# The rounded high parts of q and k made by ScalarE instead of VectorE

## The chip, the cores and the metric

The kernel runs on one core of a Trainium2 chip. The core has five engines with a queue each: TensorE (PE: matrix products, with weight loads shown apart as PEld), VectorE (DVE), ScalarE (ACT), GpSimd (POOL) and SyncE (SP), which here issues the DMA transfers. Each engine takes its instructions in the order in which they are written; between engines they wait for each other by semaphores. The metric is the device time of one execution in microseconds, as the median of several runs. One further execution was recorded by the hardware profiler; its rows carry the reasoning.

## The reference

The input x is 8 sequences of 1024 tokens with 512 features, float32. Out of one layer norm two branches are fed, and both are added to x:

```python
xn = _layernorm(x, axis=-1)
x = x + _L0_attn_ref(xn, W_attn, b_attn, W_proj, b_proj) + _L0_ffn_ref(xn, w_gate, w_up, w_down)
```

The attention has 16 heads of 32 features and is causal:

```python
qkv = x @ W_attn + b_attn
q, k, v = jnp.split(qkv, 3, axis=-1)
att = jnp.einsum('bhqd,bhkd->bhqk', q, k) * HD ** (-0.5)
att = jnp.where(causal[None, None], att, -jnp.inf)
att = jax.nn.softmax(att, axis=-1)
y = jnp.einsum('bhqk,bhkd->bhqd', att, v)
return y @ W_proj + b_proj
```

The feed-forward branch (512 to 1408 to 512) first rounds both operands of each product to 4-bit floats in blocks of 16 with a scale each: `h = silu(fp4_linear(x, w_gate)) * fp4_linear(x, w_up)`, then `fp4_linear(h, w_down)`.

## The kernel before, in words

**Tiles.** Tokens are taken in 64 tiles of 128 (class Tile). Attention is done in 64 units (class Unit): two heads (HU) of one sequence, all 1024 queries. A bank is one of six accumulators of 128x512 in PSUM (class Banks); two further accumulators, y and acc, hold sums of the attention and of the feed-forward branch.

**Stages.** `prepare` takes two tiles at a time (QT = 2): it normalises them (`normed`, VectorE and GpSimd), turns them on TensorE (`transposed`, L351; ScalarE copies the result to xnT, L352) and calls `project`. `weights_quantised` rounds the three weight matrices of the feed-forward branch and turns them; the rounding itself (class `Quantised`, L320 to L344) is on VectorE. These run at the start: the preparation of the first 16 tiles (AHEAD) beside most of the weights. After that six streams are merged until the end: `weigh` (the attention itself), `maxima` (row maxima and sums of one unit ahead), the feed-forward `network`, `quantised` (its input tiles), the remaining preparations, and `finish` (output projection and sum).

**The projection of q and k.** For each pair of tiles `project` makes, for q and for k (s), two steps of two blocks of 128 features (f): 16 products on TensorE into one bank (L466), then two ScalarE operations of 128x256 that add the bias, scale q, and write the tile `full` in SBUF (L478). So there are 4 steps for a pair and 128 in all. Each step ends with a split: q and k are kept as two parts that add up, `high` (rounded to float32r, a float32 type of fewer mantissa bits that TensorE multiplies) and `low` (the remainder, also written as float32r, over `full`). Both parts go to DRAM (`store`, L497, on SyncE), and `load_half` loads them again as `qs` and `ks`, of which the products of `maxima` (L597) and `weigh` (L727) are made. The two steps for v in `project` write their copy into a tile that is also named `full` (L522). Both `full` and `high` have two buffers (pool p2), and a buffer can be written again when the store from it has landed.

**The split.** VectorE makes `high` by a copy with conversion (L491) and then `low = full - high` (L492). The split isn't written where the step is, but later: `stored.append(Later(end - clock[0] - 0.3, split))`, where `end` is the planned end of the second ScalarE operation; `settle(stored)` in the next step writes whatever is still outstanding before a new `full` is taken. The two stores follow the same way.

**What sets the order.** The program is written out at build time by a planner. It has a clock of its own, and for ScalarE, VectorE and GpSimd a time at which each will be free (`free`). `act(columns, after)` and `dve(us, after)` add an operation to these accounts: ScalarE is charged 0.17 us and 0.00083 us per column, VectorE the number of microseconds given; `after` is the time before which the operation can't start, to which HOP = 0.2 us is added. `Later` objects are due at a planned time and are written when the clock passes it. `merge` picks the stream whose next step can start soonest, by the planned time of its inputs and by `banks.when`, the planned time at which enough banks come free. `maxima` also waits for `free["dve"] - QUEUE` (L629). So a changed charge can change the order in which the program's instructions are written, on every engine.

**Releases.** A bank used by `maxima` is released by ScalarE's exponential with a sum (L568), one used by `weigh` by the exponential L735, one of the projection by L478 or L522.

Of the kernel before, what the change touches and what calls it, by code (L numbers as in the profile page):

```python
# [27 lines left out]
def kernel(  # L28
# [31 lines left out]
    nc = tc.nc  # L60
# [14 lines left out]
    W = QG * P  # L75
# [69 lines left out]
    def on(engine, us, after=0.0):  # L145

        free[engine] = max(free[engine], clock[0], after + HOP) + us
        return free[engine]

    def act(columns, after=0.0, function="other"):  # L150
        if function == "other":
            function = table[0]
        switch = TABLE if function != table[0] else 0.0
        table[0] = function
        return on("act", 0.17 + 0.00083 * columns + switch, after)

    def dve(us, after=0.0):
        return on("dve", us, after)
# [275 lines left out]
    def settle(entries):  # L434
        while entries:
            entries.pop(0).now()
# [16 lines left out]
    def project(batch, xnT, g, after, first):  # L453
        yield 0.0, after, 1
        for s in range(2):
            for f in range(0, NC, 2):
                if first:
                    halves = [w[:, :, :] for w in resident_a[s * NC + f : s * NC + f + 2]]
                else:
                    wa = ring_a.take()  # L460
                    halves = [wa[:, :, j * P : (j + 1) * P] for j in range(2)]
                k, bank = banks.take()
                pq = bank.rearrange("p (j t) -> p j t", j=2)
                for j in range(2):
                    for c in range(NC):
                        nc.tensor.matmul(  # L466
                            pq[:, j, :],
                            lhsT=halves[j][:, c, :],
                            rhs=xnT[:, c, :],
                            start=(c == 0),  # L470
                            stop=(c == NC - 1),
                        )
                if not first:
                    ring_a.load_in(3.44 + HOP)
                settle(stored)
                full = p2.tile([P, 2, QW], F32, name="full")
                for j in range(2):
                    nc.scalar.activation(  # L478
                        full[:, j, :],
                        pq[:, j, :],  # L480
                        AF.Identity,
                        bias=bqk[:, s, f + j : f + j + 1],
                        scale=SCALE if s == 0 else 1.0,
                    )
                    end = act(QW, clock[0] + 1.7 * (j + 1))
                banks.back(k, end)
                high = p2.tile([P, 2, QW], F32R, name="high")
                low = full.bitcast(F32R)

                def split(full=full, high=high, low=low):  # L490
                    nc.vector.tensor_copy(high, full)  # L491
                    nc.vector.tensor_tensor(low, full, high.bitcast(F32), ALU.subtract)  # L492
                    dve(1.15)

                def store(s=s, f=f, high=high, low=low):
                    for piece, part in ((0, high), (1, low)):
                        nc.sync.dma_start(  # L497
                            out=batch.qk[s, piece, f : f + 2, :, g * QW : (g + 1) * QW].rearrange("f p t -> p f t"),
                            in_=part.bitcast(F32),
                        )  # L500

                stored.append(Later(end - clock[0] - 0.3, split))
                stored.append(Later(end - clock[0] + 2.0, store))
                yield 3.44, 0.0, 1
        for f in range(0, NC, 2):
            wa = resident_a[2 * NC + f // 2] if first else ring_a.take()
            k, bank = banks.take()
            pv = bank.rearrange("p (i t) -> p i t", i=QT)
            for i in range(QT):
                for c in range(NC):  # L510
                    nc.tensor.matmul(  # L511
                        pv[:, i, :],
                        lhsT=xnT[:, c, i * P : (i + 1) * P],
                        rhs=wa[:, c, :],
                        start=(c == 0),
                        stop=(c == NC - 1),
                    )
            if not first:
                ring_a.load_in(3.44 + HOP)
            settle(stored)  # L520
            v_out = p2.tile([P, QT, 2 * P], F32, name="full")
            nc.scalar.copy(v_out, pv)  # L522
            end = act(W, clock[0] + 3.44)
            banks.back(k, end)

            def store(f=f, v_out=v_out):
                nc.sync.dma_start(
                    out=batch.v[g * QT : (g + 1) * QT, :, f * P : (f + 2) * P].rearrange("t p e -> p t e"), in_=v_out
                )

            stored.append(Later(end - clock[0] + 0.5, store))
            yield 3.44, 0.0, 1
# [650 lines left out]
```

## Time and profile before

| | |
|---|---|
| median of 3 runs | 4255.48 us (4254.81 to 4258.41) |
| the profiled execution's own time | 4251.42 us |
| its span, first to last instruction | 4249.7 us |
| granted TensorE clock, mean | 0.991 |
| the 128 casts L491 | 54.8 us busy, 428 ns each |
| the 128 subtractions L492 | 89.3 us busy, 697 ns each |
| the 256 operations L478 | 107.4 us busy, 470 ns each |

The profile names an operation by its line in the kernel, its engine, and what it writes and reads ("high<-full"). "bank L597 <- ACT bank L568: 16.2, 49, 1.6" in the list of waits says that operations of line 597 stood idle before they started, until line 568 on ScalarE was done: 16.2 us in total, 49 times, 1.6 us the longest. In the timeline a row gives the start, the length, the engine, the operation and, in brackets, the idle time of the engine before it and what ended it. In the table of stretches each engine has its busy time and the number of its instructions. Idle time of an engine that isn't the bound costs nothing, and the busy time of TensorE is not a measure of its peak.

### The profile page before, as it was taken

To read this page: it belongs to the slowest core of one execution; us is meant where nothing else is said; L and a number is where in the kernel's file an instruction comes from. 1 tells how busy PE (TensorE), PEld (TensorE's weight loads), DVE (VectorE), ACT (ScalarE), POOL (GpSimd) and SP (SyncE) were. 2 spreads that over 40 slices of the span, in tenths; PEclk is the share of its full clock that TensorE was granted. 3 is DMA by queue.
4 is the path that set the end of the run, shared out by engine and by line. 5 is a ranking of instruction groups with operands and counts; after the bars stand their busy time and mean duration, and the time that the engine had idled before them with its cause. 6 is when DMAs were issued, how large, how long until landed. Compare 5 with 4: busy or idle time off the path is not lost.

```text
span 4249.7 us, 58555 instructions
## 1 busy us (share of the span) xinstructions
PE 4131.2 (97%) x17684; PEld 2619.1 (62%) x17684; DVE 2763.2 (65%) x7323; ACT 2321.8 (55%) x5918; POOL 546.5 (13%) x1296
## 2 busy tenths in 40 slices
PE   7789999999999999999999999999999999999998
PEld 6666666666666666666666666666666555555555
DVE  6786765666575666575666575666565666667755
ACT  2246556565555565555565555565555666666640
POOL 0001111111111111111111111111111111111110
PEclk9889999999999999999999999999999999999999
DMA  5654434455455455455455455455454433333314
GB/s 183 177 173 129 124 103 120 118 157 157 132 155 150 140 164 153 132 156 151 140 160 155 134 154 149 141 162 153 138 149 131 117 92 94 95 92 93 93 56 126
DMA packets 564187, 573.84 MB, mean 135 GB/s; under 512 B 114976, under 2 KB 420128, under 8 KB 563872
## 3 DMA queue, kind: packets, MB, share of 16 engines
q1 hardware_dynamic: 563872, 570.10, 48.3%
q8 instruction: 142, 2.33, 0.2%
q14 instruction: 173, 1.42, 0.1%
HBM read 400.56 MB, written 169.35 MB: 134 GB/s over the span
## 4 chain that ended last, share of the span: by engine, by line
PE 82%; ACT 7%; DVE 4%; DMA 1%; issue 1%; SPq 0%; ACTq 0%; POOL 0%; DVEq 0%
PE bank L831 26%; PE acc L809 12%; PE bank L466 8%; PE y L706 7%; PE bank L724 6%; PE bank L727 6%; PE bank L597 5%; PE bank L936 5%; PE bank L511 4%; ACT bank L568 3%; PE bank L351 2%; ACT L568 1%; ACT L843 1%; ACT pr L735 1%; DMA ks<-y_kept 1%
## 5 line engine op out<-in xcount | busy, mean ns | idle before, releaser
L568 ACT ACTIVATE bank<-bank,neg 128x512 f32<-128x512 f32 (+3 forms) x1536 | 856.7, 559 | 163.7 <-DVE neg L610 119.8
L735 ACT ACTIVATE pr<-bank 128x512 f32<-128x512 f32 (+3 forms) x1536 | 662.7, 494 | 482.6 <-PE bank L727 478.2
L741 POOL TENSOR_SCALAR_AFFINE_SELECT pr<-pr 128x128 f32<-128x128 f32 x1024 | 393.2, 397 | 3238.3 <-ACT pr L735 3228.9
L610 DVE CUSTOM_DVE_ANT_0 bank<-bank,mask 128x128 f32<-128x128 f32 (+3 forms) x1024 | 501.2, 500 | 469.5 <-PE bank L597 455.7
L724 PE MATMUL bank<-shT,pick 128*128 128x512 f32 (+3 forms) x1536 | 683.8, 453 | 2.7 <-DVE hid L848 1.5
L831 PE MATMUL bank<-wuT,xqT 128*128 128x512 f32 (+1 forms) x1536 | 676.1, 565 | 3.9 <-ACT bank L568 1.0
L809 PE MATMUL acc<-wdT,hqT 128*128 128x512 f32 x1408 | 665.4, 596 | 1.3 <-ACT hqT L352 1.3
L831 PE MATMUL bank<-wgT,xqT 128*128 128x512 f32 (+1 forms) x1536 | 662.9, 561 | 0.0
L597 PE MATMUL bank<-ks,qs 128*128 128x512 f32 (+3 forms) x1536 | 636.2, 475 | 24.7 <-ACT bank L568 21.7
L727 PE MATMUL bank<-qs,ks 128*128 128x512 f32 (+3 forms) x1536 | 516.9, 346 | 0.0
L622 DVE TENSOR_REDUCE neg<-bank 128x1 f32<-128x512 f32 x512 | 345.7, 685 | 186.8 <-PE bank L597 185.6
L597 PEld LDWEIGHTS bank<-ks,qs 128*128 128x128 f32 x1536 | 277.5, 191 | 234.1 <-issue 111.3
L831 PEld LDWEIGHTS bank<-wuT,xqT 128*128 128x128 f32 x1536 | 277.0, 190 | 228.8 <-issue 158.9
L831 PEld LDWEIGHTS bank<-wgT,xqT 128*128 128x128 f32 x1536 | 280.0, 190 | 219.3 <-issue 151.9
L724 PEld LDWEIGHTS bank<-shT,pick 128*128 128x128 f32 x1536 | 290.4, 189 | 155.7 <-issue 78.9
L809 PEld LDWEIGHTS acc<-wdT,hqT 128*128 128x128 f32 x1408 | 255.3, 190 | 197.0 <-issue 183.6
L478 ACT ACTIVATE full<-bank,bqk 128x256 f32<-128x256 f32 x256 | 107.4, 470 | 491.1 <-PE bank L466 409.3
L727 PEld LDWEIGHTS bank<-qs,ks 128*128 128x128 f32 x1536 | 290.6, 189 | 110.6 <-issue 77.1
L466 PE MATMUL bank<-xnT,wa 128*128 128x256 f32 x1536 | 349.8, 381 | 0.9 <-ACT xnT L352 0.6
L466 PEld LDWEIGHTS bank<-xnT,wa 128*128 128x128 f32 x1536 | 288.4, 190 | 55.6 <-issue 18.9
L706 PE MATMUL y<-pr,vs 128*32 128x512 f32 (+3 forms) x3072 | 316.5, 501 | 0.8 <-POOL pr L741 0.8
L568 ACT ACTIVATION_READ_ACCUMULATOR bank<-bank,neg 128x1 f32 x1536 | 315.4, 205 | 0.0
(99 smaller groups left out, 4674.7 us busy)
## 6 DMA issues: line engine op xcount, KB each, us to landing
wa<-in_L_attn_W_attn_dram SPq DMA_DIRECT2D x146, 512.0 KB
qs<-qk_kept SPq DMA_DIRECT2D x512, 128.0 KB
ks<-qk_kept SPq DMA_DIRECT2D x512, 128.0 KB
wp<-in_L_attn_W_proj_dram SPq DMA_DIRECT2D x81, 512.0 KB
qk_kept<-high SPq DMA_DIRECT2D x128, 256.0 KB
qk_kept<-full SPq DMA_DIRECT2D x128, 256.0 KB
y_kept<-yu SPq DMA_DIRECT2D x256, 128.0 KB
yT<-y_kept SPq DMA_DIRECT2D x112, 256.0 KB
```

The source lines that it names most:

```text
L466: nc.tensor.matmul(pq[:, j, :], lhsT=halves[j][:, c, :], rhs=xnT[:, c, :], start=(c == 0), stop=(c == NC - 1),)
L568: nc.scalar.activation(part, part, AF.Exp, bias=neg[:, kind, k + j : k + j + 1], scale=1.0 if kind == 1 else -1.0, accum_out=sums[:, kind, ...
L597: nc.tensor.matmul(sc[:, j * n : (j + 1) * n], lhsT=un.qs[Q][:, r, i * P : (i + 1) * P], rhs=un.ks[h][:, r, :n], start=True, stop=True,)
L610: nc.vector.tensor_tensor_reduce(part, part, mask[:, W - n :], scale=-1.0, scalar=3e38, op0=ALU.add, op1=ALU.min, accum_out=neg[:, kind, k ...
L622: nc.vector.tensor_reduce(neg[:, kind, k : k + 1], sc[:, :n], AX.X, ALU.max, negate=True)
L706: nc.tensor.matmul(y[row : row + HD, q0:], lhsT=un.vs[h][:, jj, r * HD : (r + 1) * HD], rhs=pr[:, q0:], start=(j < 2), stop=(j >= last - 1 ...
L724: nc.tensor.matmul(w[:, q0:], lhsT=pick[:, Q * HU + r, :], rhs=un.shT[:, q0:], start=True, stop=False)
L727: nc.tensor.matmul(w[:, q0:], lhsT=un.ks[h][:, r, jj * P : (jj + 1) * P], rhs=un.qs[Q][:, r, q0:], start=False, stop=True,)
L735: nc.scalar.activation(pr[:, q0:], w[:, q0:], AF.Exp)
L741: nc.gpsimd.affine_select(out=pr[:, q0 : q0 + P], in_=pr[:, q0 : q0 + P], compare_op=ALU.is_ge, fill=0.0, base=0, pattern=[[1, P]], channe ...
L809: nc.tensor.matmul(tl.acc, lhsT=job.hqT[:, j, :], rhs=wdT[:, i, :], start=(i == 0), stop=(i == NI - 1))
L831: nc.tensor.matmul(job.g, lhsT=job.tl.xqT[:, c, :], rhs=wT[:, c, job.i0 : job.i0 + job.w], start=(c == 0), stop=(c == NC - 1),)
```

## The change

The copy that makes `high` from `full` is issued on ScalarE instead of VectorE. VectorE keeps the subtraction. The planner's accounts follow: ScalarE is charged a copy of 512 columns, and VectorE 0.7 us (before: 1.15 us for both), not before 0.1 us after the planned end of the copy. Everything else, the buffers, the moment at which the split is written, and the stores, stays as it is.

```diff
@@ -488,9 +488,10 @@
                 low = full.bitcast(F32R)
 
                 def split(full=full, high=high, low=low):
-                    nc.vector.tensor_copy(high, full)
+                    nc.scalar.copy(high, full)
+                    rounded = act(W)
                     nc.vector.tensor_tensor(low, full, high.bitcast(F32), ALU.subtract)
-                    dve(1.15)
+                    dve(0.7, rounded + 0.1)
 
                 def store(s=s, f=f, high=high, low=low):
                     for piece, part in ((0, high), (1, low)):
```

## The prediction

> **What bounds the kernel now.** I read the page's busy shares first, then the span cut into five stages, then who waits for whom on TensorE, then the operations of the split itself, then the timeline at the places where TensorE stands still.
>
> The busy shares, whole span:
>
> ```profile
> PE 4131.2 (97%) x17684; PEld 2619.1 (62%) x17684; DVE 2763.2 (65%) x7323; ACT 2321.8 (55%) x5918; POOL 546.5 (13%) x1296
> ```
>
> An average hides stages, so the span in five stretches (columns: stretch, its length, then busy time of PE, PEld, DVE, ACT and POOL, the granted clock, the DMA share and GB/s):
>
> ```profile
> 0.00:330.00 330.00, 257.06 (x1204) 213.17 (x1205) 251.50 (x610) 106.40 (x270) 21.77 (x54) 0.91 0.58 174
> 330.00:700.00 370.00, 362.69 (x1559) 224.30 (x1557) 236.18 (x648) 227.80 (x595) 50.88 (x129) 0.99 0.45 124
> 700.00:3240.00 2540.00, 2529.70 (x10892) 1601.60 (x10892) 1614.02 (x4336) 1435.95 (x3668) 340.36 (x798) 1.00 0.53 147
> 3240.00:4000.00 760.00, 750.36 (x3154) 444.00 (x3153) 523.66 (x1415) 474.43 (x1213) 109.79 (x266) 1.00 0.39 99
> 4000.00:4250.00 250.00, 231.37 (x881) 135.97 (x879) 137.88 (x316) 77.24 (x175) 23.73 (x49) 0.99 0.30 86
> ```
>
> From 700 to 3240 us TensorE idles 10.3 us in 2540 (0.4%): no other engine can give more than that back there. The idle time lies at the start (72.9 us before 330, at a clock of 0.91) and at the end (18.6 us after 4000). VectorE is 76% busy before 330 and ScalarE 32%; in 700 to 3240 it is 64% and 57%.
>
> TensorE's waits before 330 us:
>
> ```profile
> PE bank L351 <- DVE hid L344: 28.7, 3, 12.8
> PE bank L351 <- DVE xt L405: 15.5, 1, 15.5
> PE bank L466 <- ACT xnT L352: 14.7, 9, 3.8
> PE bank L655 <- DVE stat L651: 4.8, 1, 4.8
> ```
>
> and from 330 to 4000 us, the longest:
>
> ```profile
> PE bank L597 <- ACT bank L568: 16.2, 49, 1.6
> PE bank L724 <- DVE hid L848: 1.3, 7, 0.2
> ```
>
> Early TensorE waits for VectorE (the quantising of weights, L335 to L344); later it waits, little, for ScalarE to release a bank. So the engine that gives work away matters early, the one that takes it matters late.
>
> The operations on the tile that is split:
>
> ```profile
> L478 ACT ACTIVATE full<-bank,bqk x256: 465/471/480, 23.8 to 3228.6; 128x256 f32<-128x256 f32 x128
> L491 DVE CAST high<-full x128: 409/422/508, 24.6 to 3229.5; 128x512 fp32r<-128x512 f32 x128
> L492 DVE TENSOR_TENSOR full<-full,high x128: 691/692/831, 25.1 to 3230.0; 128x512 fp32r<-128x512 f32 x128
> L522 ACT COPY full<-bank x64: 585/585/592, 38.5 to 3270.5; 128x512 f32<-128x512 f32 x64
> ```
>
> There are 128 splits: 36 before 330 us, 92 from 390 to 3230, none after.
>
> **What comes off VectorE.** 128 casts, 54.8 us busy. What one takes from the engine's time is the step to the subtraction behind it, which waits for it (243.88 to 244.33 us): 0.45 us. So 36 x 0.45 = 16.2 us early, 92 x 0.45 = 41.4 us later. The subtraction stays at 0.69 us.
>
> **What comes onto ScalarE.** 128 copies of 128x512. The nearest row, L522, reads PSUM and takes 0.585 us. The new one reads SBUF. The only SBUF reader on ScalarE is the exponential of 16 columns (L639, 226 ns). The slope between the PSUM copies of 128 and 512 columns (L657 254 ns, L522 586 ns) is 0.86 ns a column, so L639 plus 496 columns gives 0.65 us. Bounds 0.585 and 0.65; I take 0.65, since that row shares the source: 36 x 0.65 = 23.4 us early, 92 x 0.65 = 59.8 us later. Copies set off no table load in this trace (the loads stand at L568, L639, L735, L843 and once at the first instruction), so I add none. A load per split would be 1.28 us (L843's loads), and I exclude it.
>
> [...]
>
> **Early, before 330 us: -3.6 us.** Taken: only casts that stand in a run of VectorE work whose end TensorE waits for. The longest such wait but one:
>
> ```profile
> 164.23 0.42 DVE L491 CAST high<-full 128x512 fp32r<-128x512 f32 x1
> ...
> 168.42 0.42 DVE L491 CAST high<-full 128x512 fp32r<-128x512 f32 x1
> ...
> 171.60 0.68 DVE L344 TENSOR_TENSOR hid<-hid,scale 128x512 f32<-128x512 f32 x1
> ...
> 172.43 1.09 PE L351 MATMUL bank<-ident,hid 128*128 128x128 f32 x4 [11.70 <-DVE hid L344]
> ```
>
> Two casts, 0.9 us, of an 11.7 us wait; the rest is the input's DMA (VectorE had waited 14.06 us for xt until 162.2) and the quantising itself. The same count: for the 12.8 us wait that ends at 134.3, two casts (112.28, 117.41) stand before the stores and the load of hid that it comes from, 0.9 us; for the 3.76 us wait that ends at 179.3 (a ScalarE copy behind a store of full), the cast at 172.80, 0.45; for the 4.1 us wait that ends at 259.2, the casts at 239.14, 243.88 and 250.34, 1.35. Sum 3.6. Bounds: 0, if subtractions wait for ScalarE as long as the casts took; 16.2, if every cast lies on the path. The cover for the 36 copies is ScalarE's idle time (it sits 47.5 us before L478 until L466 ends); without it they cost 23.4 us.
>
> **Middle, 330 to 3240 us: +3.5 us.** ScalarE goes from 56.5% to about 58.6%. Behind the copy on its queue stand the exponentials that release banks (L568) and make weights (L735). TensorE waits 10.1 us for L568 here. Upper bound by load: from 3240 to 4000, where nothing is projected, ScalarE is 62.4% busy and TensorE idles 1.27%; 2.1 of the 5.9 points' difference times 0.87% of 2900 us is 8.8 us. Lower bound: a gain of the 1.3 us that TensorE waits for VectorE in this stretch. I take 3.5, near the middle, because that denser stretch also has VectorE at 69%, which the change lowers.
>
> **The new wait.** The subtraction now waits for ScalarE's copy, with the next VectorE work behind it (a row minimum or a quantising step, for which a bank's release or a transposition waits). The cast had such a wait already: 28 times, 131.1 us, for L478 in the middle stretch. Where VectorE came early, the subtraction's end moves from 0.45 + 0.69 to 0.65 + 0.69 us after L478, 0.2 us late, plus whatever ScalarE has queued in between; where it came late (64 of 92), it is 0.45 us early. The buffer of the high part brings no new wait: it is freed by the store before the one that frees full, and L478 in front of the copy waits for that.
>
> **Queues.** No DMA is added. SyncE waits 284.8 us in all for the cast before it stores the high part; that store now waits for ScalarE, usually earlier, and the low part's store shifts by the 0.2 late or 0.45 early. Loads of the rings queue behind it; I count nothing, since TensorE waits for no ring in the trace; one store held 0.5 us longer would cost at most that.
>
> **The planner.** Its account changes: ScalarE is charged 0.59 us more; VectorE's account ends 0.75 us later where it is idle (copy 0.595 + 0.1 + HOP 0.2 + 0.7 against 1.15) and 0.45 us earlier where it is full. That shifts when maxima and banks count as ready, so the written order will differ here and there. I price this at 0 with +-6 us, the size of half an early wait; the steady rate of idle, 0.4%, hardly differs between stretches with different orders.
>
> **The end, from 3240 us: 0.** No split lies there.
>
> **Sum.** 4249.7 (span) - 3.6 + 3.5 = 4249.6; the profiled execution took 4251.4, 1.7 us round its span, and the median of the runs is 4255.5, 4.1 us above that. So 4255.4 us: a balance.
>
> **Rivals.**
> 1. Faster: VectorE is the whole bound of the start. For: 28.7 us of TensorE's wait there end with it, and it is 83% busy from 200 to 300 us. Then all 16.2 us come off: 4255.4 - 12.6 = 4242.8; with clock regained, less. Against: the two longest waits begin with a DMA.
> 2. Slower, the other side: ScalarE becomes the releaser that TensorE waits for. If a share of the 59.8 us reaches TensorE by late L568 and L735, it decides from 15 us (the 3.6 gained, the 8.5 of the margin and some more): a quarter. At 30%: 4255.4 - 3.5 + 17.9 = 4269.8. For: 49 waits on L568 already. Against: they are 0.3 us each, and ScalarE itself waits 478.2 us for TensorE at L735.
> 3. Slower on VectorE: each subtraction that comes early waits behind two exponentials (2 x 0.76 us, activation plus accumulator read) as well as the copy. 28 x 1.7 = 48 us on VectorE, of which a wait for L848 would pass on a few: with a tenth, 4260. It stays within the margin.
>
> **Chances.** A change of 0.2% (8.5 us) is about what a measurement of this kernel can tell from none. Balance, rival 3 in it: 0.50, its own range 4248 to 4263. Rival 2 and an order that came out worse: 0.28. Rival 1 and an order that came out better: 0.22. The range runs from rival 1 and a bit of the order's 6 us (4241) to rival 2 at a little over a third of the copies (4273).
>
> **What would show it.** Right: the cast gone from VectorE, about 41 us less there in the middle; 128 copies on ScalarE near 0.65 us, no more table loads; the three waits for hid before 330 us shorter by some 0.9 to 1.35 us each; TensorE's idle time in 700 to 3240 between 9 and 17 us; the end unchanged. Wrong: waits for L568 that multiply in the middle; one of the 12 us early waits gone or a new one there, because the order changed; a granted clock other than 0.91 at the start.

## The result and the profile after

The changed kernel takes 4317.61 us (median, 4313.6 to 4319.7), the kernel before 4255.45 us beside it: a ratio of 1.0144 with a 95% interval of 1.0126 to 1.0161. It is 62 us slower, against a forecast of no change and a range that ended at 4273. The profiled execution took 4318.91 us, its span is 4317.2 us.

The busy shares of the changed kernel, over the whole span:

```profile
PE 4168.7 (97%) x17684; PEld 2629.2 (61%) x17684; DVE 2702.1 (63%) x7195; ACT 2383.3 (55%) x6046; POOL 537.3 (12%) x1296
```

VectorE does 61 us less and ScalarE 62 us more, as meant. TensorE has the same 17684 products and is shown busy for 37.5 us longer.

The same five stretches of the changed kernel (columns as in the table of before: stretch, length, busy time of PE, PEld, DVE, ACT, POOL, granted clock, DMA share, GB/s):

```profile
0.00:330.00 330.00, 263.19 (x1223) 217.98 (x1224) 242.39 (x592) 128.78 (x314) 23.13 (x54) 0.91 0.60 177
330.00:700.00 370.00, 361.49 (x1543) 221.85 (x1542) 227.35 (x622) 234.82 (x611) 49.69 (x129) 0.99 0.44 121
700.00:3240.00 2540.00, 2496.84 (x10623) 1570.37 (x10625) 1535.40 (x4154) 1433.83 (x3651) 323.72 (x779) 0.99 0.52 143
3240.00:4000.00 760.00, 748.75 (x3137) 443.58 (x3130) 507.66 (x1381) 466.33 (x1186) 106.44 (x256) 0.99 0.40 102
4000.00:4320.00 320.00, 298.49 (x1171) 175.39 (x1169) 189.31 (x448) 119.51 (x287) 34.35 (x78) 0.99 0.33 90
```

Before 330 us TensorE gets through more work than before (1223 products against 1204). From 700 to 3240 us it gets through less: 10623 products against 10892, and it idles 43.2 us where it idled 10.3. That is the stretch in which I allowed +3.5 us.

TensorE's waits in the changed kernel before 330 us (each: waiting line, what it waited for, us in total, times, longest):

```profile
PE bank L351 <- DVE hid L344: 17.0, 3, 8.6
PE bank L351 <- DVE xt L405: 15.6, 1, 15.6
PE bank L466 <- ACT xnT L352: 12.5, 9, 3.7
```

and from 330 to 4000 us (the code's lines stand one lower than before, so L598 and L569 are L597 and L568 of before):

```profile
PE bank L598 <- ACT bank L569: 45.0, 92, 1.6
PE bank L598 <- ACT hqT L352: 8.4, 19, 0.4
```

The waits for hid, the longest for VectorE at the start, fell from 28.7 to 17.0 us. The products of the row maxima now wait 45.0 us for an exponential to release a bank, against 16.2.

The operations of the split in the changed kernel:

```profile
L491 ACT CAST high<-full x128: 606/626/649, 24.7 to 3291.6; 128x512 fp32r<-128x512 f32 x128
L493 DVE TENSOR_TENSOR full<-full,high x128: 678/691/694, 25.4 to 3292.3; 128x512 fp32r<-128x512 f32 x128
```

The copy takes 0.626 us; my bounds were 0.585 and 0.65.

**Where in the cycle the time goes.** In the middle the written order repeats itself after two units of attention. These are TensorE's waits for an exponential in three repetitions in a row. Before, they are all:

```profile
1585.33 0.49 PE L597 MATMUL bank<-ks,qs 128*128 128x512 f32 x1 [0.17 <-ACT bank L568]
1713.11 0.49 PE L597 MATMUL bank<-ks,qs 128*128 128x512 f32 x1 [0.17 <-ACT bank L568]
1840.89 0.50 PE L597 MATMUL bank<-ks,qs 128*128 128x512 f32 x1 [0.17 <-ACT bank L568]
```

After, the first repetition has three, and each of the next two begins with the same long one (the rows behind it are left out):

```profile
1605.39 0.50 PE L598 MATMUL bank<-ks,qs 128*128 128x512 f32 x1 [1.22 <-ACT bank L569]
1606.06 0.50 PE L598 MATMUL bank<-ks,qs 128*128 128x512 f32 x1 [0.17 <-ACT bank L569]
1606.72 0.50 PE L598 MATMUL bank<-ks,qs 128*128 128x512 f32 x1 [0.17 <-ACT bank L569]
...
1735.69 0.50 PE L598 MATMUL bank<-ks,qs 128*128 128x512 f32 x1 [1.22 <-ACT bank L569]
...
1865.98 0.50 PE L598 MATMUL bank<-ks,qs 128*128 128x512 f32 x1 [1.23 <-ACT bank L569]
```

The period is 127.8 us before (1585.33 to 1713.11 to 1840.89) and 130.3 after. Measured by the copy to xnT that begins a pair of tiles, it is 127.8 us in each of the last 18 periods before; after, these are 131.8 and 132.3 and then 130.3, 130.3, 132.0 in turn. From the fourteenth pair of tiles (866.7 us before, 868.8 after) to the last, the 32nd (3166.7 and 3226.1), that is 2300.0 and 2357.3 us: 57.3 us in 18 periods, of the 67.5 by which the spans differ. The two periods ahead of it (242.4 us before, 247.7 after) bring 5.3, and what follows the last pair brings 8.1; at the twelfth pair (624.3 and 621.1) the changed kernel still leads by 3.2.

What happens there is seen on ScalarE. The same stretch before (the exponentials of the row maxima are L568, the pair of Silu operations is L843, each change between the two a table load of 1.28 us):

```profile
1578.37 0.70 ACT L568 ACTIVATE bank<-bank,neg 128x512 f32<-128x512 f32 x1
...
1579.05 0.47 ACT L568 ACTIVATE bank<-bank,neg 128x256 f32<-128x256 f32 x1
...
1579.66 0.45 ACT L568 ACTIVATE bank<-bank,neg 128x256 f32<-128x256 f32 x1
...
1580.25 1.28 ACT L843 ACT_TABLE_LOAD   x1
```

and after:

```profile
1599.31 0.67 ACT L569 ACTIVATE bank<-bank,neg 128x512 f32<-128x512 f32 x1
...
1600.59 1.28 ACT L844 ACT_TABLE_LOAD   x1
1601.88 0.98 ACT L844 ACTIVATE hid<-bank 128x512 f32<-128x512 f32 x2
1602.88 1.28 ACT L569 ACT_TABLE_LOAD   x1
1604.17 0.45 ACT L569 ACTIVATE bank<-bank,neg 128x256 f32<-128x256 f32 x1
```

Before, the two exponentials of 256 columns are written ahead of the Silu pair; after, behind it. Counted from the pair's table load they start 4.8 us later (3.58 us behind it instead of 1.20 ahead), TensorE waits 1.22 us for a bank, and the last three products of the unit then follow 0.67 us apart, the pace of the exponentials, where 0.23 us is the step of such products when the bank is there (those that start at 2043.07, 2043.30, 2043.53 and 2043.77 us). None of the 128 copies stands in this stretch: it is the order that differs here. One period differs by 1.8 us of visible idle time (2.0 us, with a 0.44 us wait earlier in the period, against 0.17).

### The profile page after: what moved, and what is told of

It is laid out like the page before. It is cut to its first block, busy times and chain, and to the rows that moved or that the text cites. A ratio compares the mean times of both kernels' runs of the same rounds, so it can differ in the third digit from the quotient of the medians.

```text
span 4317.2 us, 58530 instructions
## 1 busy us (share of the span) xinstructions
PE 4168.7 (97%) x17684; PEld 2629.2 (61%) x17684; DVE 2702.1 (63%) x7195; ACT 2383.3 (55%) x6046; POOL 537.3 (12%) x1296
## 4 chain that ended last, share of the span: by engine, by line
PE 82%; ACT 6%; DVE 3%; DMA 2%; issue 1%; SPq 1%; POOL 0%; ACTq 0%; DVEq 0%; POOLq 0%
PE bank L832 26%; PE acc L810 12%; PE bank L466 9%; PE y L707 7%; PE bank L725 6%; PE bank L728 6%; PE bank L598 5%; PE bank L512 5%; PE bank L937 5%; ACT bank L569 3%; PE bank L351 2%; ACT L569 1%; DMA ks<-y_kept 1%; ACT hid L844 1%; DVE neg L623 1%
## 5 line engine op out<-in xcount | busy, mean ns | idle before, releaser
L569 ACT ACTIVATE bank<-bank,neg 128x512 f32<-128x512 f32 (+3 forms) x1536 | 858.1, 561 | 176.1 <-DVE neg L611 132.5
L742 POOL TENSOR_SCALAR_AFFINE_SELECT pr<-pr 128x128 f32<-128x128 f32 x1024 | 384.1, 388 | 3322.7 <-ACT pr L736 3313.7
L598 PE MATMUL bank<-ks,qs 128*128 128x512 f32 (+3 forms) x1536 | 625.9, 469 | 58.2 <-ACT bank L569 46.2
L598 PEld LDWEIGHTS bank<-ks,qs 128*128 128x128 f32 x1536 | 279.5, 190 | 271.2 <-issue 99.5
L478 ACT ACTIVATE full<-bank,bqk 128x256 f32<-128x256 f32 x256 | 107.3, 470 | 492.5 <-PE bank L466 355.5
L569 ACT ACTIVATION_READ_ACCUMULATOR bank<-bank,neg 128x1 f32 x1536 | 317.2, 207 | 0.0
```

The lines of the kernel that those rows point to most:

```text
L569: nc.scalar.activation(part, part, AF.Exp, bias=neg[:, kind, k + j : k + j + 1], scale=1.0 if kind == 1 else -1.0, accum_out=sums[:, kind, ...
L598: nc.tensor.matmul(sc[:, j * n : (j + 1) * n], lhsT=un.qs[Q][:, r, i * P : (i + 1) * P], rhs=un.ks[h][:, r, :n], start=True, stop=True,)
L742: nc.gpsimd.affine_select(out=pr[:, q0 : q0 + P], in_=pr[:, q0 : q0 + P], compare_op=ALU.is_ge, fill=0.0, base=0, pattern=[[1, P]], channe ...
```

## The experiments

All ratios are to the kernel before on the same chip, with 95% intervals. The first four take the change apart: the engine that copies on one side, the planner's accounts on the other.

**The copy with the old accounts.** TensorE's, GpSimd's and SyncE's written orders are exactly those of before; ScalarE has the copies in addition.

```diff
-                    nc.vector.tensor_copy(high, full)
+                    nc.scalar.copy(high, full)
                     nc.vector.tensor_tensor(low, full, high.bitcast(F32), ALU.subtract)
                     dve(1.15)
```

> The copy is on ScalarE, but the planner's account of the split stays as it was (VectorE 1.15 us, ScalarE nothing), so that the written order of TensorE's instructions is exactly that of the kernel before. Theory O (the loss comes from the written order that the new accounts brought): within 10 us of before, 4245 to 4265, with the 0.4% of idle TensorE in the steady stretch. Theory L (the loss comes from ScalarE's 80 us of added work itself): 4300 to 4325, with waits of L597 for L568 near the 46 us of after.

4257.69 us, 1.000 (0.9991 to 1.001). The move itself costs nothing that can be measured (0.1% is 4 us). TensorE's waits from 330 to 4000 us and the middle stretch:

```profile
PE bank L597 <- ACT bank L568: 16.6, 50, 1.6
700.00:3240.00 2540.00, 2529.59 (x10892) 1599.06 (x10893) 1570.41 (x4254) 1475.57 (x3746) 337.19 (x798) 1.00 0.53 147
```

The waits for an exponential are those of before (16.2), and the period is 127.8 us as before, though VectorE now waits 240.2 us for ScalarE at the subtraction (before: 147.0 at the cast).

**The cast with the new accounts.** TensorE's written order is exactly that of the changed kernel.

```diff
                     nc.vector.tensor_copy(high, full)
+                    rounded = act(W)
                     nc.vector.tensor_tensor(low, full, high.bitcast(F32), ALU.subtract)
-                    dve(1.15)
+                    dve(0.7, rounded + 0.1)
```

> The cast stays on VectorE, but the accounts are those of the changed kernel, so that TensorE's order is exactly that of after. Theory O: 4300 to 4320, waits of L598 for L569 over 30 us in all. Theory L: 4250 to 4265, those waits near 20 us.

4328.18 us, 1.0169 (1.0153 to 1.0184). No engine does other work than before, and the kernel is as slow as the changed one, or slower. The waits for exponentials from 330 to 4000 us:

```profile
PE bank L598 <- ACT bank L569: 44.6, 89, 1.6
PE bank L598 <- ACT hqT L352: 8.4, 19, 0.4
```

These are the waits of the changed kernel (45.0 and 8.4), and the periods are its too (130.3, 130.3, 132.0). Theory O, the written order, stands, and theory L, the load on ScalarE, falls.

**ScalarE's charge alone, and VectorE's account alone**, both with the cast on VectorE:

```diff
-                    dve(1.15)
+                    act(W)
+                    dve(1.15)
```

> The cast stays on VectorE; of the accounts only ScalarE's charge of 0.595 us for each split is added, VectorE's 1.15 us stays. If order is what counts and ScalarE's charge (banks counted as free later) is the part that spoils it: 4300 or more. If VectorE's account is the part: 4245 to 4270. Theory L: as before, 4250 to 4262.

```diff
-                    dve(1.15)
+                    rounded = max(free["act"], clock[0], HOP) + 0.17 + 0.00083 * W
+                    dve(0.7, rounded + 0.1)
```

> The cast stays on VectorE; of the accounts only VectorE's is changed (0.7 us, not before ScalarE's planned free time plus 0.695), ScalarE is charged nothing. If order counts and VectorE's later account is the part that spoils it: 4300 or more. If ScalarE's charge is the part: 4245 to 4270. If any change of an account throws the order into a worse one, both this and the run with ScalarE's charge alone lie above 4275. Theory L: 4250 to 4262.

ScalarE's charge alone: 4248.55 us, 0.9977 (0.9968 to 0.9987), period 127.4 us. VectorE's account alone: 4367.48 us, 1.0258 (1.0243 to 1.0273), period 133.1 us. So the loss comes by VectorE's account. It changes in two ways: the charge falls from 1.15 to 0.7, and the subtraction waits, in the plan, for ScalarE's planned end (the waiting term).

**The two ways apart**, with the copy on ScalarE and its charge, and a check on chance:

```diff
 # copy on ScalarE, ScalarE's charge only
+                    act(W)
                     dve(1.15)
 # copy on ScalarE, both charges, no waiting term
+                    act(W)
-                    dve(1.15)
+                    dve(0.7)
 # copy on ScalarE, waiting term, the old charge
+                    rounded = act(W)
-                    dve(1.15)
+                    dve(1.15, rounded + 0.1)
 # the kernel before with one number changed
-                    dve(1.15)
+                    dve(1.25)
```

> The copy on ScalarE and ScalarE's charge of 0.595 us, VectorE's account as it was (1.15 us, no waiting): the written order of the cast with ScalarE's charge alone (which took 0.9977 of before), with the engine moved. If the move itself is free, as the run with the copy and the old accounts showed (1.000): 4244 to 4256, a ratio of 0.996 to 1.000.

4247.89 us, 0.9978 (0.9968 to 0.9987): the order of the cast with ScalarE's charge alone, with the engine moved; the move is free again.

> The copy on ScalarE, ScalarE's charge, VectorE charged 0.7 us without the waiting term. If the waiting term of VectorE's account is what spoils the order: 4240 to 4265. If the smaller charge (0.7 for 1.15) spoils it: over 4300. If any change of these accounts draws an order by chance: anywhere from 4245 to 4370.

4240.31 us, 0.9961 (0.9947 to 0.9974): the fastest of all, faster than both kernels. It is the change as made, without `rounded + 0.1`.

> The copy on ScalarE, ScalarE's charge, VectorE charged the old 1.15 us but with the waiting term (not before ScalarE's planned end plus 0.1). If the waiting term spoils the order: 4300 to 4370. If the smaller charge does: 4240 to 4265. By chance: anywhere between.

4303.97 us, 1.0108 (1.0092 to 1.0123). The waiting term spoils the order with either charge, 0.7 or 1.15.

> The kernel before with one number of the plan changed, VectorE's charge for the split 1.25 us instead of 1.15; no engine's work differs. If a later VectorE account as such spoils the order: slower by up to 0.3%, much less than the waiting term, which adds up to 0.75 us. If the order is thrown by any change: as far off as the others, over 1% in either direction.

4248.9 us, 0.9978 (0.9969 to 0.9987). Neither expectation was met. A tenth of a microsecond in the plan of a split, and no difference in the work, moves the kernel by 0.2%, here to the better: even so small a change of an account draws a new order, but what it moved is less than the 0.5 to 2.6% that the runs with the waiting term lose.

The fastest of these in its middle stretch:

```profile
700.00:3240.00 2540.00, 2527.26 (x10927) 1603.10 (x10925) 1582.55 (x4262) 1487.62 (x3763) 308.53 (x798) 1.00 0.54 148
```

and its waits of TensorE from 330 to 4000 us:

```profile
PE bank L598 <- ACT bank L569: 17.7, 38, 1.1
PE bank L832 <- ACT bank L569: 6.1, 22, 0.3
```

ScalarE is 58.6% busy there, the share that I had worked out, and TensorE still does 10927 products in the stretch, 35 more than before. The load that I feared is no bound.

**Who reads the account.** VectorE's planned time is read by the gate of the row maxima (`free["dve"] - QUEUE`), as the end of a row minimum (which places its exponential and says when its bank comes free), and as the end of the quantising, gating and normalising steps. Two accounts were kept, one with and one without the waiting term, and the readers divided between them:

```diff
     def on(engine, us, after=0.0):
+        if engine == "dve":
+            free["gate"] = max(free["gate"], clock[0], after + HOP) + us
...
-                    dve(0.7, rounded + 0.1)
+                    plain = max(free["gate"], clock[0], HOP) + 0.7
+                    dve(0.7, rounded + 0.1)
+                    free["gate"] = plain
...
-            yield cost, free["dve"] - QUEUE, 1
+            yield cost, free["gate"] - QUEUE, 1
```

> The changed kernel, with one difference: the gate of the row maxima (the planned VectorE time less QUEUE) reads a second VectorE account that leaves out the waiting term of the split; everything else that is planned on VectorE keeps the term. If the gate is how the waiting term spoils the order: 4235 to 4265, a period of two units near 127.5 us. If it is the planned ends of VectorE's operations (from which banks and exponentials are placed): 4295 to 4370.

4310.97 us, 1.0127 (1.011 to 1.0144).

The mirror, where `free["gate"]` gets the waiting term and `free["dve"]` doesn't:

> The mirror of it: only the gate of the row maxima reads the account with the waiting term; all else is planned without. If the gate is the way: 4295 to 4370, periods of 130 us or more. If the planned ends are: 4235 to 4265.

4276.05 us, 1.0047 (1.0032 to 1.0062), period 128.7 us. Then the gate was given back to `free["dve"]`, and the row minima read the second account instead (`end = free["gate"]` behind their `dve(...)`), once without the term where all else has it, once with it where nothing else has:

> The changed kernel, in which only the planned ends of the row minima (from which the exponentials are placed and banks counted as free) are read from the account without the waiting term; the gate, the quantising, the gated products and the normalisation keep it. If the minima's ends are the main way: 4250 to 4280 (the gate alone gave 1.0047). If the other ends (quantising, gating) are: 4290 to 4330.

4293.39 us, 1.0087 (1.007 to 1.0104).

> The mirror: only the planned ends of the row minima carry the waiting term, all else including the gate is planned without. If the minima's ends are the main way: 4290 to 4330. If the other ends are: 4240 to 4270. If both lie near 4280, no single reader of the account carries it and each delay spoils the order by a part.

4302.99 us, 1.0108 (1.0093 to 1.0123). No single reader carries it: gate alone 0.5%, row minima alone 1.1%, all but the row minima 0.9%, all together 1.4%. The parts don't add up; each draws an order of its own, so there is no reason that they should.

**A shorter waiting term.**

```diff
-                    dve(0.7, rounded + 0.1)
+                    dve(0.7, rounded - 0.6)
```

> The changed kernel with a waiting term that is 0.7 us shorter (not before ScalarE's planned end less 0.6), so that where VectorE is idle in the plan its account ends 0.05 us later than in the kernel before instead of 0.75. If the size of the delay is what counts: 4240 to 4265. If any waiting for ScalarE's account (which can lie far ahead when exponentials are queued) does it: 4290 or more.

4289.65 us, 1.0079 (1.0064 to 1.0094), period 128.8 and 130.5 in turn: half the loss with a term 0.7 us shorter. Neither expectation was met: more than the first, a little less than the second. Size counts, but a term that leaves VectorE's account only 0.05 us later than before, where VectorE is idle in the plan and ScalarE has nothing further planned, still costs 0.8%.

Taken together: the changed kernel and the eight others whose plan lets VectorE's account wait for ScalarE's, in whole or in part, lie between 1.005 and 1.026, with 21.5 to 44.3 us of idle TensorE from 700 to 3240 us. The kernel before and the five without the term lie between 0.996 and 1.000, with 10.3 to 12.7 us. The same wait marks them in the traces: from 330 to 4000 us the products of the row maxima wait 32.7 to 45.4 us for their exponentials in the nine, and 13.8 to 17.7 us in the six.

## Why the prediction was wrong

**The term that failed** is "I price this at 0 with +-6 us", the planner. It is +62 us and, with the copy moved for nothing, the whole of the result. The reason I gave, that "the steady rate of idle, 0.4%, hardly differs between stretches with different orders", was a misreading. The 0.4% is that of the middle, and the middle is one cycle of 127.8 us, written 18 times: the trace of before showed one order there, not a sample of them. Outside it, by the prediction's own table, the rate is 2.0% from 330 to 700 us and 1.3% from 3240 to 4000. A loss of 3.2 us in the cycle (57.3 over 18) comes 18 times. Two of the signs that I had named did come: the waits for L568 multiplied, and TensorE's idle time from 700 to 3240 us was 43.2 us, not 9 to 17. The 0.75 us in that step is the right size, but the terms beside it add up to 0.445; the other 0.3 is that the split is written 0.3 us ahead of the planned end of L478.

**The rivals.** Rival 1 isn't borne out: with the old accounts the four early waits gave back 3.6 us, not 16.2. Rival 2 named the right wait (L568 releasing banks), but priced it at 4269.8, 14 us up where 62 came, and for a reason that the first run refutes: the same copies in the old order leave that wait at 16.6 us. "An order that came out worse" was in its chance, without a price. Rival 3, subtractions that hold up VectorE, isn't borne out by the same run: 240 us of waiting at the subtraction, and no loss beyond the 0.1% of its interval.

**What comes off VectorE, what comes onto ScalarE:** right. 0.626 us for a copy (0.65 taken), no more table loads (188 in each profile), 54.8 us of casts gone.

**Early, -3.6 us:** the sum was right in the unchanged order, the places weren't. In the run with the old accounts the four waits went from 12.84, 11.70, 3.76 and 4.14 us to 12.16, 8.90, 3.62 and 4.16: 3.6 us together, but 2.8 of them at the second, where I had counted 0.9, and nothing at the fourth, where I had counted 1.35; that the sum agreed is luck. At the ninth pair 2.2 us were left (its products begin at 284.84 instead of 287.00). Part of the gain went to the clock: two groups of 32 products ran 9.04 and 9.83 us, instead of 7.17 and 8.60 us at a granted clock of 1.00 and 0.83; from these lengths (7.17 us at 1.00) I estimate 0.79 and 0.73 for the run. In the new order the start gained too: 6.8 us at the eleventh pair (495.4 instead of 502.2), of which the twelfth kept 3.2.

**Middle, +3.5 us:** too pessimistic for the work itself (and its upper bound comes to 9.0 us by the terms given, not 8.8). In the run with the old accounts the stretch from the eleventh pair of tiles (502.2 us before, 500.8 in that run) to the last took 2665.7 us instead of 2664.5, +1.2. The exponentials behind a copy have room: ScalarE waits 445.4 us for TensorE at L735 in that run.

**The sum.** 4255.4 us was forecast, and the kernel that has the engines of the change and the order of before takes 4257.7. The forecast was right for another kernel than the changed one, and as a balance alone: its two terms, -3.6 and +3.5, are smaller than the 4 us to which the total can be told.

**What stays open.** Shown is that the waiting term does it, through more than one reader, and that in the changed kernel exponentials then stand behind the Silu pair and TensorE waits for their banks. Why a plan that tells the truth about VectorE (the subtraction does wait, 229.0 us in all) gives a worse order than one that leaves it out isn't shown. I had taken orders to differ by chance; four orders without the term and eight with it, each on its own side of 1.002, speak for a bias, not only for chance, though the eight have the term in common and aren't independent draws; the runs don't say where in the planner it lies. Nor was a fixed charge as long as the waiting term tried: only 0.1 us more was, so whether it is the wait for ScalarE's account or merely a VectorE account that ends much later isn't separated. That the short term still loses 0.8% speaks for the wait.

## What to carry to other kernels

Where a planner writes the program out, the charges in its accounts are part of the change: build the kernel once with the new work and the old accounts and once the other way round, before the work is blamed. A steady middle that repeats one cycle is one sample of the order, so its low idle time says nothing of the next order; what a new order loses in one cycle it loses in every repetition, here 3.2 us 18 times. A truer account isn't a better order by itself: with `dve(0.7)` alone, the same move is 0.4% faster than the kernel before, by its order, since the move is free.

## What the runs showed of the hardware

TensorE's granted clock fell to 0.50 with no gap over 1.23 us. In the changed kernel the stretch with the three waits is followed by 16 products (L512) that take 3.72 us in two repetitions and 5.41 us in the third. The third's row:

```profile
1475.31 5.41 PE L512 MATMUL bank<-wa,xnT 128*128 128x256 f32 x16
```

The 3.5 us in front of it and the 10 us that hold both (columns as in the table of stretches):

```profile
1472.30:1475.80 3.50, 2.00 (x5) 1.03 (x6) 3.19 (x8) 3.47 (x13) 0.00 (x0) 1.00 0.19 75
1470.00:1480.00 10.00, 8.38 (x25) 5.41 (x24) 5.35 (x15) 7.76 (x21) 0.00 (x0) 0.83 0.07 26
```

The longest single wait there is 1.23 us, but TensorE is busy for only 2.00 us of 3.5. In the trace the granted clock is 0.50 from 1476.01 to 1479.43 us and 1.00 on both sides: 3.4 us at half clock are 1.7 us less, and the 16 products take 1.7 us longer. In the kernel before it doesn't fall between 380 and 3790 us. The drop explains the period of 132.0 after two of 130.3; spread over three it is 0.6 us of the 3.1 that a period loses on the mean (130.9 against 127.8). The visible idle time is 1.8 of them. The rest I put down to rows like L598's 0.50 us, which are longer than the 0.23 us by which such products follow each other when the bank is there; that is an argument and was not measured by itself, and a few such rows stand in the kernel before as well.

The drop comes again at 1868.55 and 2261.08 us: 392.5 us each time, three periods, and it lasts 3.4 us each time. Why only every third repetition has one isn't shown: in the 3.5 us ahead of the drop TensorE is busy for 2.00 us, and in the same 3.5 us of the repetitions ahead of it and behind it (from 1342.00 and from 1604.30 us), after which the clock stays at 1.00, for 1.95 and 2.02 us.
